# Two bottleneck blocks in f32: the centre taken off behind TensorE's transposes, and VectorE's steps in the Gram stages cut smaller

## The chip, the cores and the metric

The kernel runs on one core of one Trainium2 chip. The metric is the device time of one execution in microseconds (us), and of several executions the median.

## What is computed

The reference applies two residual bottleneck blocks, one behind the other, to x of 64 x 1024 x 14 x 14 in float32. One block is:

```python
out = relu(_bn(_conv(x, w1, b1, 1, 0), g1, be1))      # 1x1, 1024 -> 256
out = relu(_bn(_conv(out, w2, b2, 1, 1), g2, be2))    # 3x3, 256 -> 256
out = _bn(_conv(out, w3, b3, 1, 0), g3, be3)          # 1x1, 256 -> 1024
out = softplus(residual_scale)[0] * out
out = relu(x + out)
```

`_bn` is a batch norm with the mean and variance of the batch itself, over images and pixels. So each block needs the statistics of every convolution's output before it can go on. For the third convolution the kernel doesn't form all outputs twice: their mean and variance follow from the mean of its 256 input channels and from their 256 x 256 matrix of second moments (the Gram matrix), taken over all 64 x 196 = 12544 pixels.

## The kernel before

All 256 channels of the middle tensor, y, lie in SBUF: 128 partitions, two slots (s = 0, 1) of 12544 pixels. A block runs in stages: first convolution, second convolution, the Gram stage (`gram`), statistics of the third convolution (`conv3_stats`), then the third convolution with the residual, in the first block interleaved with the next block's first convolution. TensorE (PE) multiplies, ScalarE (ACT) evicts and applies the norm, VectorE (DVE) adds, GpSimd (POOL) adds and issues some DMAs, SyncE (SP) issues the other DMAs.

The change touches `gram` alone, which runs once per block. It has to do three things for each pixel: apply the second norm and the ReLU in place (`norm` on ScalarE, or `norm_vector` in two steps on VectorE), take off a guess of the channel's mean (`less`: `minus_c`, one number per channel, is added; sums of squares are more exact about a centre), and bring pixels from the free dimension to the partitions, since TensorE contracts over partitions. A transposed pair of chunks, 256 pixels by 256 channels, goes into a tile `zt` (six in turn, each with a column of ones for the mean), and four matmuls into the banks `cp` (g0) and `ap` (g1) add its products. There are 49 pairs, and two ways to transpose one:

- `by_tensor(a)`: four TensorE transposes into a PSUM bank, then VectorE copies the bank to `zt` (line 1046). This serves the first `FIRST` = 7 pairs, while no other data is ready.
- `by_vector(x, i)`: VectorE's stream transpose turns blocks of 32 x 32 (line 1052). The blocks have to lie right first, so DMAs spread 1536 pixels (a step) over a second buffer, a home: 16 DMAs a step, four runs of pixels by four groups of partitions, seven on POOL's queue and nine on SP's (line 1032). There are two homes, used in turn (named `ws` and `home` in the first block's trace, both `home` in the second's), and seven steps of six pairs each. Step 0 takes the pixels 768 to 2303, so that TensorE's pairs 3 to 6 take those from 2304 on.

Pair i's matmuls stand behind the transposes of pair i + 1 in PE's program. PE, DVE and ACT execute in the order in which the program lists their instructions; here the order is written out by hand (`tc.keep_in_program_order`). `pairs` lists it: after the pairs 1 and 5 of TensorE the steps 0 and 1 are spread, after step k the step k + 2, into the same home. `norm_to(end)` norms and centres whole pieces of pixels up to `end`, mostly 1568 long, whenever a spread needs them; so six stream transposes stand in a row on VectorE, and then two `less` of 1568. A pad matmul (`busy`, into the bank `ax`) stands behind the first pair's transposes.

Of the kernel before, what the change touches and what calls it, by code (L numbers as in the profile page):

```python
# [52 lines left out]
NPX = N * HW  # L53
CH = 2
NZT = 6

FIRST, LAST = 7, 0
RUN = 3 * P
STEP = 4 * RUN
STEPS = (NPX - (FIRST + LAST) * CH * P) // STEP  # L60

LAG = 14

# [3 lines left out]
GPX = GI * HW  # L67
# [20 lines left out]
def bottlenecks(ctx: ExitStack, tc: tile.TileContext, x, w1s, w2s, w3s, pars, out):  # L88
    nc = tc.nc
# [5 lines left out]
    y_all = keep.tile([P, MS, NPX], FP, tag="y", name="y")  # L95
# [70 lines left out]
    def matmul(*args, **kw):  # L166

        tc.keep_in_program_order(nc.tensor.matmul(*args, **kw))  # L168

    def busy(psum, tag, n, with_=None):  # L170

        v = ident if with_ is None else with_
        for i in range(n):
            matmul(psum.tile(448, tag), v, v[:, :1].to_broadcast([P, 448]), start=True, stop=True)
# [154 lines left out]
    def act(*args, **kw):  # L329

        tc.keep_in_program_order(nc.scalar.activation(*args, **kw))  # L331
# [662 lines left out]
    def gram(psum, pool, homes, aff, minus_c, beside):  # L994

        g0, g1 = psum.tile(M + 1, "cp"), psum.tile(P + 1, "ap")
        zts = [pool.tile([P, CH, M + 1], FP, tag=f"zt{i}", name=f"zt{i}") for i in range(NZT)]
        for zt in zts:  # L1000
            nc.gpsimd.memset(zt[:, :, M:], 1.0)
        zts = itertools.cycle(zts)

        head = 3 * CH * P
        start = FIRST * CH * P
        bounds = [0, CH * P, head, head + STEP, *range(2 * GPX, NPX + 1, GPX)]
        pieces = list(zip(bounds, bounds[1:]))

        def less(s, y):
            tc.keep_in_program_order(nc.vector.tensor_scalar(y, y, minus_c[:, s : s + 1], None, ALU.add))  # L1010

        def norm_to(end):

            while pieces and pieces[0][0] < end:
                a, e = pieces.pop(0)
                for s in reversed(range(MS)):
                    y = y_all[:, s, a:e]
                    if a == 0 and s == 1:
                        norm_vector(s, y, aff, minus_c[:, s : s + 1])
                    else:  # L1020
                        norm(s, y, aff)
                        less(s, y)

        def spread(k):

            first = start + k * STEP if k else head
            norm_to(first + STEP)
            x = homes[k % 2][:, : MS * STEP].rearrange("p (s j f) -> p s j f", s=MS, j=4)
            for i, j in itertools.product(range(4), range(4)):
                queue = nc.gpsimd if 4 * i + j in (1, 3, 6, 8, 10, 13, 15) else nc.sync  # L1030
                a = first + i * RUN
                queue.dma_start(out=x[32 * i : 32 * i + 32, :, j], in_=y_all[32 * j : 32 * j + 32, :, a : a + RUN])
            return x.rearrange("p s j f -> p (s j) f")

        def by_tensor(a):
            tp = psum.tile(CH * M)
            for c in range(CH):
                for s in range(MS):
                    tc.keep_in_program_order(
                        nc.tensor.transpose(  # L1040
                            tp[:, (c * MS + s) * P : (c * MS + s + 1) * P],
                            y_all[:, s, a + c * P : a + (c + 1) * P], ident,
                        )
                    )
            zt = next(zts)
            tc.keep_in_program_order(nc.vector.tensor_copy(zt[:, :, :M], tp.rearrange("p (c m) -> p c m", c=CH)))  # L1046
            return zt

        def by_vector(x, i):
            zt = next(zts)  # L1050
            tc.keep_in_program_order(
                nc.vector.transpose(
                    zt[:, :, :M].rearrange("p b (n c) -> p b n c", c=32),
                    x[:, :, i * CH * 32 : (i + 1) * CH * 32].rearrange("p n (b r) -> p b n r", r=32),
                )
            )
            return zt

        def pairs():

            norm_to(head)
            then = {
                1: lambda: ready.append(spread(0)),
                2: partial(norm_to, 2 * GPX),
                4: partial(norm_to, 3 * GPX),
                5: lambda: ready.append(spread(1)),
            }
            for i in range(FIRST):
                a = i * CH * P
                yield by_tensor(a if a < head else a + STEP)  # L1070
                if i == 0:
                    busy(psum, "ax", 1)
                if i in then:
                    then[i]()
            for k in range(STEPS):
                x = ready.pop(0)
                for i in range(RUN // (CH * 32)):
                    yield by_vector(x, i)
                if k + 2 < STEPS:
                    ready.append(spread(k + 2))  # L1080
            norm_to(NPX)
            for i in range(LAST):
                yield by_tensor(NPX - (LAST - i) * CH * P)

        ready = []
# [239 lines left out]
    ident = keep.tile([P, P], FP, tag="ident", name="ident")  # L1325
# [6 lines left out]
    with tc.tile_pool(name="first", bufs=1) as one, tc.tile_pool(  # L1332
        name="first_x", bufs=4
    ) as xpool, ExitStack() as scope:
        psum = Psum(scope, ["ps"], ps=4, ay=2)
        w1 = load_w1(one, 0, nc.scalar)
        pair = [load_x(xpool, 0, t, CS if t == 0 else 2) for t in range(2)]
        for b in range(2):
            p = keep.tile([P, NPAR], FP, tag=f"par{b}", name=f"par{b}")
# [14 lines left out]
        pieces = list(itertools.product(range(2), range(MS), range(MS)))  # L1354
# [16 lines left out]
    for b in range(2):  # L1371
        pb = par[b]
        minus_c = keep.tile([P, MS], FP, tag="minus_c", name="minus_c")
# [5 lines left out]
        with tc.tile_pool(name=f"last_{b}", bufs=1) as one, tc.tile_pool(  # L1379
            name=f"last_x_{b}", bufs=4 if b == 0 else 5  # L1380
# [4 lines left out]
            aff = affine(aggregate(stats2, 0), pb, G2, BE2)  # L1385
            with ExitStack() as scope:
                if b == 0:
                    psum = Psum(scope, ["cy", "ay", "cx", "cy", "ay"], cy=2, ay=2)
                else:
                    psum = Psum(scope, ["cy", "cx"], cy=2, cx=2, cp=2)  # L1390
                with tc.tile_pool(name=f"gram_{b}", bufs=1) as pool:
                    def x_tile(name):
                        return xpool.tile([P, CS * PX], FP, tag="x", name=name)
# [3 lines left out]
                    homes = [x_tile("home") if b else ws.rearrange("p i n -> p (i n)"), x_tile("home")]  # L1397
# [17 lines left out]
                aff = affine(mv3, pb, G3, BE3, conv_bias=B3)  # L1415
# [51 lines left out]
```

## Time and profile before

| | us |
|---|---|
| median of 3 runs (1943.93 to 1944.21) | 1944.0 |
| profiled execution, its own time | 1944.06 |
| profiled execution, its span | 1942.3 |
| first Gram stage: from the norm's first step on ACT to the last Gram matmul | 586.49 to 659.93 |
| second Gram stage, the same | 1552.01 to 1624.91 |

The span is the time from the first to the last instruction on the core. The page of the profile gives the busy time of each engine, the chain of work that ended last, the costliest groups of instructions and the DMA issues. Other views used here are the groups by line and shape, the waits of an engine (who waited for whom, total, times, longest), the timeline (start, duration, engine, line, operation, tiles, shapes, count, and in brackets the idle time before and what ended it) and busy times in stretches. A row of the timeline with xN stands for N instructions in a row.

### The profile page before, as it was taken

How to read it: one execution, taken by the hardware profiler on the slowest of the kernel's cores; microseconds unless marked ns; L12 is line 12 of the kernel's file. 1: busy time of each engine (PE TensorE's matmuls, PEld its weight loads, DVE VectorE, ACT ScalarE, POOL GpSimd, SP SyncE). 2: the span in 40 equal slices, each digit the busy share in tenths (PEclk: the TensorE clock that was granted, in tenths of full speed). 3: DMA queues.
4: the chain of work that ended last, by engine and by line, in shares of the span. 5: the costliest groups of instructions: out<-in, count | busy, mean ns of one | idle time of the engine just before them, and what ended most of it. 6: DMA issues, size and time to landing. Idle time of an engine off the chain costs nothing.

```text
span 1942.3 us, 27081 instructions
## 1 busy us (share of the span) xinstructions
PE 1918.6 (99%) x9438; PEld 1612.1 (83%) x9438; DVE 1544.3 (80%) x2473; ACT 1046.2 (54%) x2098; POOL 575.1 (30%) x674
## 2 busy tenths in 40 slices
PE   9999999999999999999999999999999999999999
PEld 5555557999997799999999999989999987555555
DVE  5778667999998667776776767689999975888886
ACT  2222214677765055555555555456777651666666
POOL 0111100212105133433333334302121051666664
PEclk9999999999999999999999999999999999999999
DMA  7777634887948634444444444258788486899998
GB/s 291 273 250 263 235 129 157 204 221 202 230 141 207 197 137 187 175 166 166 181 185 167 166 178 180 108 181 209 215 208 225 140 194 233 279 334 335 333 342 300
DMA packets 201849, 413.91 MB, mean 213 GB/s; under 512 B 37809, under 2 KB 178001, under 8 KB 185201
## 3 DMA queue, kind: packets, MB, share of 16 engines
q1 hardware_dynamic: 161728, 324.66, 49.0%
q0 software_dynamic: 34368, 36.45, 9.3%
q10 hardware_dynamic: 5616, 51.06, 6.3%
q8 instruction: 75, 1.23, 0.3%
q14 instruction: 62, 0.50, 0.1%
HBM read 263.75 MB, written 115.34 MB: 195 GB/s over the span
## 4 chain that ended last, share of the span: by engine, by line
PE 92%; DVE 5%; DMA 1%; ACT 1%; issue 1%; SPq 0%; POOL 0%; DVEq 0%; ACTq 0%
PE cy L168 17%; PE ay L168 17%; PE columns L168 13%; PE cp L168 12%; PE ap L168 10%; PE m L168 6%; PE l L168 6%; PE cx L168 5%; PE ax L168 4%; PE ps L168 1%; DMA home<-y 1%; ACT y L544 1%; DVE v L628 0%; DVE sums L622 0%; DVE steps L697 0%
## 5 line engine op out<-in xcount | busy, mean ns | idle before, releaser
L331 ACT ACTIVATE cu<-cy,scale 128x196 f32<-128x196 f32 (+1 forms) x552 | 256.7, 474 | 277.5 <-PE cy L168 271.3
L168 PE MATMUL columns<-v,ub 128*128 128x224 f32 (+1 forms) x1536 | 300.7, 337 | 0.0
L331 ACT ACTIVATE x<-x,shift 128x392 f32<-128x392 f32 x428 | 241.1, 613 | 59.5 <-POOL x L490 53.1
L168 PEld LDWEIGHTS columns<-v,ub 128*128 128x128 f32 x1536 | 269.2, 188 | 2.8
L464 DVE SCALAR_TENSOR_TENSOR x<-cp,scale,x 128x196 f32<-128x196 f32 (+1 forms) x368 | 178.2, 484 | 97.2 <-PE cp L168 96.1
L168 PE MATMUL cy<-ct,ws 128*128 128x196 f32 (+1 forms) x736 | 221.9, 383 | 1.1 <-ACT cu L331 1.1
L485 POOL TENSOR_TENSOR x<-x,cu 128x196 f32<-128x196 f32 (+1 forms) x184 | 159.3, 866 | 172.1 <-ACT cu L331 162.5
L168 PE MATMUL ay<-at,ws 128*128 128x196 f32 (+1 forms) x752 | 209.1, 381 | 0.0
L490 POOL TENSOR_TENSOR x<-x,cu 128x392 f32<-128x392 f32 x124 | 125.9, 1016 | 192.8 <-DVE x L464 188.1
L168 PEld LDWEIGHTS ay<-at,ws 128*128 128x128 f32 x752 | 136.5, 190 | 33.4
L168 PEld LDWEIGHTS cy<-ct,ws 128*128 128x128 f32 x736 | 133.3, 190 | 36.4 <-ACT cu L331 4.2
L168 PE MATMUL l<-diffs,ub 128*128 128x224 f32 (+1 forms) x768 | 149.1, 337 | 2.6 <-PE columns L168 2.6
L511 POOL TENSOR_TENSOR x<-x,cu 128x392 f32<-128x392 f32 x120 | 121.9, 1017 | 85.9 <-DVE x L464 62.4
L168 PE MATMUL m<-sums,ua 128*128 128x224 f32 (+1 forms) x752 | 145.9, 337 | 1.5 <-DVE sums L622 1.5
L168 PEld LDWEIGHTS l<-diffs,ub 128*128 128x128 f32 x768 | 134.3, 189 | 4.4 <-PE columns L168 3.9
L331 ACT ACTIVATE au<-ay 128x196 f32<-128x196 f32 (+1 forms) x141 | 53.8, 381 | 155.2 <-PE ay L168 152.4
L464 DVE SCALAR_TENSOR_TENSOR x<-cx,scale,x 128x196 f32<-128x196 f32 (+1 forms) x184 | 89.1, 484 | 57.4 <-PE cx L168 57.4
L168 PEld LDWEIGHTS m<-sums,ua 128*128 128x128 f32 x752 | 131.3, 189 | 3.3 <-DVE sums L622 2.9
L168 PE MATMUL cx<-y,w 128*128 128x196 f32 (+1 forms) x404 | 124.1, 392 | 0.4 <-DVE x L1148 0.4
L168 PE MATMUL cy<-y,w 128*128 128x196 f32 (+1 forms) x404 | 123.8, 392 | 0.0
L168 PE MATMUL cp<-zt 128*128 128x257 f32 x392 | 118.0, 382 | 1.8 <-DVE zt L1046 1.7
L168 PE MATMUL cp<-y,ws 128*128 128x196 f32 (+1 forms) x368 | 113.6, 390 | 0.9 <-DVE x L464 0.9
(216 smaller groups left out, 3924.8 us busy)
## 6 DMA issues: line engine op xcount, KB each, us to landing
x<-in_x SPq DMA_DIRECT2D x62, 1568.0 KB, 6.8
ub<-u SPq DMA_DIRECT2D x94, 768.0 KB, 5.2
x<-mid SPq DMA_DIRECT2D x32, 1568.0 KB, 8.2
mid<-x ACTq DMA_DIRECT2D x31, 1568.0 KB, 5.1
out<-x SPq DMA_DIRECT2D x123, 392.0 KB, 5.7
ua<-u SPq DMA_DIRECT2D x94, 256.0 KB, 3.0
u<-y POOLq DMA_DIRECT2D x48, 256.0 KB, 5.8
home<-y SPq DMA_DIRECT2D x90, 96.0 KB, 4.3
```

Source lines behind the costliest of these rows:

```text
L168: tc.keep_in_program_order(nc.tensor.matmul(*args, **kw))
L331: tc.keep_in_program_order(nc.scalar.activation(*args, **kw))
L464: nc.vector.scalar_tensor_tensor(v, bank, self.scale[:, o : o + 1], v, ALU.mult, ALU.add)
L485: nc.gpsimd.tensor_add(self.part(1, 1), self.part(1, 1), u3)
L490: nc.gpsimd.tensor_add(v, v, self.u12)
L511: nc.gpsimd.tensor_add(v, v, self.u12[:, i * self.n : (i + 1) * self.n])
L544: act(y, y, AF.Relu, bias=shift[:, s : s + 1], scale=scale[:, s : s + 1])
```

## The change

Only `gram` and the constant `LAST`, which was 0 and goes, are edited. The pieces of pixels that are normed and centred are cut differently and put elsewhere in the order:

- TensorE transposes its pairs before they are centred. Two new matmuls and a copy make `c_row`, a tile that holds `minus_c` as a row on all partitions, and VectorE's copy of the bank becomes an addition of that row. The pixels of these pairs are centred in y itself later, during the steps 1 and 2.
- Step 0 is normed, centred and spread in two halves (`move(0, range(2))`, `move(0, range(2, 4))`). Slot 1 of the pixels of TensorE's pairs 3 to 6 is normed by VectorE, in two pieces of 512.
- Pieces are steps of 1536 pixels. During step k, `less` for the step k + 2 stands behind the first and the second stream transpose, slot 1 and slot 0, instead of both behind the sixth. The `less` of the pixels that TensorE transposed stand behind the third and the fourth transpose of steps 1 and 2. `move(k + 2)` still stands behind the sixth.

The new code with its order, cut to that:

```diff
-        bounds = [0, CH * P, head, head + STEP, *range(2 * GPX, NPX + 1, GPX)]
-        def norm_to(end):
-            while pieces and pieces[0][0] < end:
-                a, e = pieces.pop(0)
-                for s in reversed(range(MS)):
-                    y = y_all[:, s, a:e]
-                    if a == 0 and s == 1:
-                        norm_vector(s, y, aff, minus_c[:, s : s + 1])
-                    else:
-                        norm(s, y, aff)
-                        less(s, y)
...
+        def center_row():
+            ps = psum.tile(M, "ax")
+            for s in range(MS):
+                matmul(
+                    ps[:, s * P : (s + 1) * P], minus_c[:, s : s + 1].to_broadcast([P, P]), ident, start=True, stop=True
+                )
+            tc.keep_in_program_order(nc.vector.tensor_copy(c_row, ps))
...
-            tc.keep_in_program_order(nc.vector.tensor_copy(zt[:, :, :M], tp.rearrange("p (c m) -> p c m", c=CH)))
+            tc.keep_in_program_order(
+                nc.vector.tensor_add(
+                    zt[:, :, :M], tp.rearrange("p (c m) -> p c m", c=CH), c_row[:, None, :].to_broadcast([P, CH, M])
+                )
+            )
...
-            norm_to(head)
-            then = {
-                1: lambda: ready.append(spread(0)),
-                2: partial(norm_to, 2 * GPX),
-                4: partial(norm_to, 3 * GPX),
-                5: lambda: ready.append(spread(1)),
-            }
+            at = head + STEP
+            half = (start + STEP - at) // 2
+            normed_by_vector(0, px, 1)
+            normed(0, px, (0,))
+            center_row()
+            normed(px, head)
+            def then(i):
+                if i == 0:
+                    busy(psum, "ax", 1)
+                elif i == 1:
+                    normed(head, middle)
+                    less(head, middle, (1,))
+                elif i == 2:
+                    less(head, middle, (0,))
+                    move(0, range(2))
+                    normed(at, at + half, (0,))
+                    normed_by_vector(at, at + half, 1)
+                    normed(middle, at)
+                elif i == 3:
+                    less(middle, at)
+                    move(0, range(2, 4))
+                    normed(at + half, start + STEP, (0,))
+                    normed_by_vector(at + half, start + STEP, 1)
+                elif i == 4:
+                    normed(start + STEP, start + 2 * STEP)
+                elif i == 5:
+                    less(start + STEP, start + 2 * STEP)
+                    move(1, range(4))
...
                 for i in range(RUN // (CH * 32)):
                     yield by_vector(x, i)
+                    a = start + (k + 2) * STEP
+                    if i < MS and k + 2 < STEPS:
+                        normed(a, a + STEP, both[i : i + 1])
+                        less(a, a + STEP, both[i : i + 1])
+                    elif 2 <= i < 2 + MS and k in (1, 2):
+                        less(*((0, head), (at, start + STEP))[k - 1], (i - 2,))
                 if k + 2 < STEPS:
-                    ready.append(spread(k + 2))
+                    move(k + 2, range(4))
```

`px` is 256, `head` 768, `middle` 1536, `start` 1792, `at` 2304 and `half` 512. `normed` calls `norm` on ScalarE for the given slots, slot 1 first; `normed_by_vector` calls `norm_vector` for one slot.

More of the change, by code (lines that the diff above doesn't have):

```diff
@@ L55 @@
 NZT = 6
-FIRST, LAST = 7, 0
+FIRST = 7
 RUN = 3 * P
 STEP = 4 * RUN
-STEPS = (NPX - (FIRST + LAST) * CH * P) // STEP
+STEPS = (NPX - FIRST * CH * P) // STEP
 LAG = 14
@@ L1002, in gram @@
         zts = itertools.cycle(zts)
-        head = 3 * CH * P
-        start = FIRST * CH * P
-        bounds = [0, CH * P, head, head + STEP, *range(2 * GPX, NPX + 1, GPX)]
-        pieces = list(zip(bounds, bounds[1:]))
-        def less(s, y):
-            tc.keep_in_program_order(nc.vector.tensor_scalar(y, y, minus_c[:, s : s + 1], None, ALU.add))
-        def norm_to(end):
-            while pieces and pieces[0][0] < end:
-                a, e = pieces.pop(0)
-                for s in reversed(range(MS)):
-                    y = y_all[:, s, a:e]
-                    if a == 0 and s == 1:
-                        norm_vector(s, y, aff, minus_c[:, s : s + 1])
-                    else:
-                        norm(s, y, aff)
-                        less(s, y)
@@ L1024, in spread, with normed, normed_by_vector, less @@
-        def spread(k):
+        px = CH * P
+        head = 3 * px
+        start = FIRST * px
+        middle = head + STEP // 2
+        both = tuple(reversed(range(MS)))
+        def normed(a, e, slots=both):
+            for s in slots:
+                norm(s, y_all[:, s, a:e], aff, act)
+        def normed_by_vector(a, e, s, less=0.0):
+            norm_vector(s, y_all[:, s, a:e], aff, less)
+        def less(a, e, slots=both):
+            for s in slots:
+                y = y_all[:, s, a:e]
+                tc.keep_in_program_order(nc.vector.tensor_scalar(y, y, minus_c[:, s : s + 1], None, ALU.add))
@@ L1026, in spread, with home, move @@
+        def home(k):
+            return homes[k % 2][:, : MS * STEP].rearrange("p (s j f) -> p s j f", s=MS, j=4)
+        def move(k, runs):
             first = start + k * STEP if k else head
-            norm_to(first + STEP)
-            x = homes[k % 2][:, : MS * STEP].rearrange("p (s j f) -> p s j f", s=MS, j=4)
-            for i, j in itertools.product(range(4), range(4)):
+            for i, j in itertools.product(runs, range(4)):
                 queue = nc.gpsimd if 4 * i + j in (1, 3, 6, 8, 10, 13, 15) else nc.sync
@@ L1031, in spread @@
                 a = first + i * RUN
-                queue.dma_start(out=x[32 * i : 32 * i + 32, :, j], in_=y_all[32 * j : 32 * j + 32, :, a : a + RUN])
-            return x.rearrange("p s j f -> p (s j) f")
+                queue.dma_start(
+                    out=home(k)[32 * i : 32 * i + 32, :, j], in_=y_all[32 * j : 32 * j + 32, :, a : a + RUN]
+                )
+        c_row = pool.tile([P, M], FP, tag="c_row", name="c_row")
+        def center_row():
[5 more added lines that the diff above has]
+            tc.keep_in_program_order(nc.vector.tensor_copy(c_row, ps))
@@ L1045, in by_tensor @@
             zt = next(zts)
-            tc.keep_in_program_order(nc.vector.tensor_copy(zt[:, :, :M], tp.rearrange("p (c m) -> p c m", c=CH)))
+            tc.keep_in_program_order(
+                nc.vector.tensor_add(
+                    zt[:, :, :M], tp.rearrange("p (c m) -> p c m", c=CH), c_row[:, None, :].to_broadcast([P, CH, M])
+                )
+            )
             return zt
@@ L1059, in pairs @@
         def pairs():
-            norm_to(head)
-            then = {
-                1: lambda: ready.append(spread(0)),
-                2: partial(norm_to, 2 * GPX),
-                4: partial(norm_to, 3 * GPX),
-                5: lambda: ready.append(spread(1)),
-            }
-            for i in range(FIRST):
-                a = i * CH * P
-                yield by_tensor(a if a < head else a + STEP)
+            at = head + STEP
+            half = (start + STEP - at) // 2
+            normed_by_vector(0, px, 1)
@@ L1071, in pairs @@
+            normed(0, px, (0,))
+            center_row()
+            normed(px, head)
+            def then(i):
                 if i == 0:
                     busy(psum, "ax", 1)
-                if i in then:
-                    then[i]()
+                elif i == 1:
[17 more added lines that the diff above has]
+                    move(1, range(4))
@@ L1075, in pairs @@
+            for i in range(FIRST):
+                a = i * px
+                yield by_tensor(a if a < head else a + STEP)
+                then(i)
             for k in range(STEPS):
-                x = ready.pop(0)
+                x = home(k).rearrange("p s j f -> p (s j) f")
                 for i in range(RUN // (CH * 32)):
                     yield by_vector(x, i)
-                if k + 2 < STEPS:
-                    ready.append(spread(k + 2))
-            norm_to(NPX)
-            for i in range(LAST):
-                yield by_tensor(NPX - (LAST - i) * CH * P)
@@ L1085, in gram @@
-        ready = []
+                    a = start + (k + 2) * STEP
[4 more added lines that the diff above has]
+                        less(*((0, head), (at, start + STEP))[k - 1], (i - 2,))
+                if k + 2 < STEPS:
+                    move(k + 2, range(4))
         total = NPX // (CH * P)
```

## The prediction

> **What bounds the kernel now.** First the page: which engine has no idle time, and whose work the chain that ended last consists of.
>
> ```profile
> PE 1918.6 (99%) x9438; PEld 1612.1 (83%) x9438; DVE 1544.3 (80%) x2473; ACT 1046.2 (54%) x2098; POOL 575.1 (30%) x674
> ...
> PE 92%; DVE 5%; DMA 1%; ACT 1%; issue 1%; SPq 0%; POOL 0%; DVEq 0%; ACTq 0%
> ```
>
> TensorE (PE) sets the time. An edit to the two Gram stages (584 to 660 us and 1550 to 1625 us) can only win PE's idle time there. So second, PE's waits in 582 to 660:
>
> ```profile
> PE cy L1040 <- DVE y L1010: 1.4, 1, 1.4
> PE cp L168 <- DVE zt L1046: 0.8, 1, 0.8
> PE cy L1040 <- PE m L168: 0.5, 1, 0.5
> ```
>
> The second stage gives the same three numbers: 2.7 us per stage. Not all can be won. A pair of transposed chunks costs PE 1.31 us (in the chain: cp 0.43 and ap 0.22, twice), six pairs (one step through a home buffer) 7.88 us. Third, the timeline of VectorE (DVE) behind the last TensorE pair, and SP's beside it:
>
> ```profile
> 602.53 3.68 DVE L1052 STREAM_TRANSPOSE zt<-ws 128x512 f32<-128x512 f32 x6
> 606.13 1.94 DVE L1010 TENSOR_SCALAR y<-y,minus_c 128x1568 f32<-128x1568 f32 x2
> 611.24 3.68 DVE L1052 STREAM_TRANSPOSE zt<-home 128x512 f32<-128x512 f32 x6 [3.17 <-DMA home<-y]
> 614.85 1.94 DVE L1010 TENSOR_SCALAR y<-y,minus_c 128x1568 f32<-128x1568 f32 x2
> 619.48 3.68 DVE L1052 STREAM_TRANSPOSE zt<-ws 128x512 f32<-128x512 f32 x6 [2.69 <-DMA home<-y]
> 623.08 1.94 DVE L1010 TENSOR_SCALAR y<-y,minus_c 128x1568 f32<-128x1568 f32 x2
> 625.43 3.71 DVE L1052 STREAM_TRANSPOSE zt<-home 128x512 f32<-128x512 f32 x6 [0.41 <-DMA ws<-y]
> ```
> ```profile
> 592.71 6.30 SPq L1032 DMA_DIRECT2D ws<-y  x9
> 599.51 6.32 SPq L1032 DMA_DIRECT2D home<-y  x9
> 606.24 6.48 SPq L1032 DMA_DIRECT2D ws<-y  x9
> 614.95 6.21 SPq L1032 DMA_DIRECT2D home<-y  x9
> ```
>
> Here lies a second bound, just under PE: each step's DMAs start 0.1 us after the sixth transpose that read the same home (614.95 after 611.24 + 3.68). Home to home again, the loop is 611.24 to 625.43 = 14.2 us (step 1 to 3), 619.48 to 633.83 = 14.4 (2 to 4); in the second stage 14.8 (1576.02 to 1590.84) and 15.0 (1582.54 to 1597.52). PE needs 15.76 for two steps: the margin is 0.8 to 1.6 us. The subtractions (1.94 us) come behind the sixth transpose, beside the DMAs, and lengthen the loop by nothing.
>
> **What the Trainium skill says.** "VectorE: DVE Perf Modes", Mode 2×_2P: an f32 tensor_scalar in SBUF makes two results a cycle, an operand in PSUM forbids it. The trace agrees: a subtraction of 1536 takes 1.02 us, the copy of 512 out of PSUM 0.69. "SBUF — State Buffer", in the box on DVE blocking DMA: GpSimd can't write DMA descriptors during such a two-port operation. It agrees: POOL's issues take 539 ns in the median and up to 1357 ns, the long ones beside subtractions. "DMA: Bandwidth & Descriptors", Issuing engines are not separate DMA queues: all queues share 16 engines. The windows from 596 to 616 show a DMA share of 1.05 to 1.10 at 203 to 232 GB/s.
>
> **The change, part by part** (times of the first stage; the second is the same 965.5 us later).
>
> 1. *Subtraction leaves the first pair's path.* Before, PE's first transposes (587.79) waited for L1010 after pads that ended at 587.32 (583.76 + 3.56). Now PE first makes the center row there: two matmuls of 128 columns at 0.22 (the row ap, 129 columns) = 0.44, to 587.76; transposes 0.44. DVE copies the row out: 0.43 (the row g<-cp, 257 columns), starting some 0.26 behind the matmul as the copies do behind transposes, to 588.45. The pad matmul writes the same bank ax and now waits for that copy, which it didn't before; with it queue the second pair's transposes: 588.5 + 0.76 = 589.3, where they were at 589.08. The first Gram matmul comes at 589.75 (589.72 before). Gain 0; bounds -0.3 to +0.3.
>
> 2. *tensor_add in place of the copy.* The same 512 elements at one per cycle; the row f<-columns,ls (896 elements, 1.09 us) scales to 0.69. Cost 0, within 0.1 either way.
>
> 3. *Pair 3.* Before: transposes at 594.45, behind four subtractions. Now DVE does add 2 (to 592.45), a subtraction of 768 (0.53 start to start, from 832 at 0.56), then two tensor_scalars on 512 (0.49 each) that norm and are new on DVE: to 593.95. PE starts at 594.0: 0.45 won, 1.2 us of wait left.
>
> 4. *Pairs 4 to 6.* The subtractions of 2 x 0.95 ahead of pairs 5 and 6 shrink to one such block. Adding up, Gram pair 6 starts at 601.45 instead of 602.63: 1.2 us won per stage, if nothing else binds. That is what the restructured norm buys; ScalarE, 512-wide pieces earlier, stays busy to about 611 and off the path.
>
> 5. *Transfers.* Order on SP (63 per stage) and POOL (49) is unchanged, only waits move. The first home: half its DMAs go at 593.0 (behind the subtraction of 768; 592.71 before), the rest at 596.45, SP being busy till then; its last issue is at 598.4 as before, so the first stream transpose stays near 602.7. Gram pair 7: 603.45 against 603.94. Of 1.2, 0.5 is left. The second home waits for a whole 1536 subtracted: 600.8 against 599.51. From issue to transpose took 11.7 here and 10.7 in the second stage (from POOL's 1565.30); POOL is no longer beside subtractions. I take 611.9 for step 1 (611.24 before), bounds 611.2 to 612.6.
>
> 6. *Subtractions between transposes.* Now two of 1536 stand between the first three transposes of steps 0 to 4, two of 768 more in step 1, two of 1024 in step 2. So the sixth transpose ends later by 1.9 us (two at 0.95), in step 1 by 1.9 + 2 x 0.53 = 2.9, in step 2 by 1.9 + 2 x 0.65 = 3.2. Behind it, on SP and POOL, queue all 16 DMAs for that home. The cover of the old subtractions was the DMA time; it is gone. Loops: steps 1 to 3 become 14.2 + 2.9 = 17.1 (17.7 in the second stage), 2 to 4 17.6 to 18.2, against PE's 15.76. Less overlap of homes lets the engines serve one faster; what that gives back no row shows. Lower bound 0, upper 1.5 (steps 4 to 6, the least crowded, took 13.5 and 14.1); I take 0.7.
>  So step 3 comes at 611.9 + 17.1 - 0.7 = 628.3, in the second stage at 611.6 + 17.7 - 0.7 = 628.6 on this clock. Its first pair follows 0.75 later: 629.05 and 629.35. Where PE is starved, the two interleaved subtractions delay the next two pairs (0.6 + 0.95 + 0.67 is over PE's 1.31): 0.2 + 0.24 = 0.44. With 24 pairs to go (31.5) the stage ends at 661.0 and 661.3, against 659.93 and 659.4 (1624.91): +1.1 and +1.9. The later homes stay just inside: step 4 by 636.5, its first pair, 0.75 behind, due at 637.4.
>
> Sum: +3.0 us. The profiled execution took 1944.06 (span 1942.3 and 1.8 around it); the median of the three runs shown is 1944.0. So 1947.0. What I can call a difference here is about 0.2%, 3.9 us.
>
> **Rivals.**
> *A, the forecast (0.58):* the home loop becomes the bound for one round: +1 to +6, so 1945 to 1950. For: the loop's margin of 0.8 to 1.6 is less than the 2.9 to 3.2 added. Against: PE was 2.0 us behind step 3's transposes here (25th pair due at 628.1), and the DMA's give-back is unknown.
> *B, the other side (0.22):* the lighter DMA traffic gives back 1.5 us or more per loop, landing never starves PE, and the head's 1.2 per stage stays, with 0.5 for the wait at 620 that step 2's landing causes in the first stage: -2.9, so 1941.1; at most -3.9 if part 1 also wins 0.5 per stage. It decides at step 3: transposes by 627 mean B. For: loops of 13.2 to 13.5 late in the stages. Against: SP alone needs 6.3 us for nine issues, and a landing 4.5.
> *C (0.14):* no give-back, and steps 4 to 6 are late too; 3.5 per stage: 1951.
> *D (0.06):* gains and losses cancel; the change doesn't do what it says for PE: 1944 to 1945.
>
> **Chances.** Slower by over 0.2% (1947.9): 0.4 of A (0.23) and C: 0.37. Faster by over 0.2% (1940.1): a quarter of B, 0.05, and 0.02 for an error in part 5. The rest, 0.56, within. A's own range is 1945 to 1950; the range for 8 in 10 takes in half of B and most of C: 1942.5 to 1951.
>
> **What would show it.** In the changed profile: Gram pair 6 by 601.5; PE's wait in pair 3 down to about 1.2 us; nine SP issues of step 3 starting about 618 instead of 614.95; PE waiting on stream transposes (not on copies or adds) near 612 and 629; POOL's 1357 ns issues gone. It is wrong if SP's step 3 starts before 616, if PE never waits behind 605, or if the stage ends outside 659 to 663.

## The result and the profile after

The changed kernel takes 1947.03 us (median of 20 runs, 1946.13 to 1949.68). The kernel before, run beside it, takes 1944.22 (20 runs, 1943.23 to 1944.86). The ratio is 1.0017, 95% interval 1.0010 to 1.0024: 2.8 us slower. The whole interval lies above 1, though most of it under the 0.2% that the prediction calls a difference. The profiled execution of the changed kernel took 1948.1, which is 1.1 above its median; the last view of this section shows a likely reason. Everything read from traces here, tables too, is from one profiled execution of each kernel.

First the page, busy time and the chain that ended last:

```profile
PE 1923.1 (99%) x9446; PEld 1615.5 (83%) x9446; DVE 1546.3 (79%) x2485; ACT 1045.3 (54%) x2102; POOL 572.6 (29%) x674
...
PE 92%; DVE 4%; DMA 2%; issue 1%; SPq 1%; ACT 0%; POOL 0%; DVEq 0%; ACTq 0%
```

TensorE still sets the time, but in the chain DVE and ACT have each lost one per cent, and DMA and SP's queue each gained one. Second, what PE waits for, in 582 to 662 (first Gram stage; from here on "the first stage") and then in 1542 to 1632 (the second); the columns are total, times and longest:

```profile
PE cp L168 <- DVE zt L1067: 1.1, 2, 0.9
PE cy L1051 <- DVE y L552: 0.8, 1, 0.8
```
```profile
PE cp L168 <- DVE zt L1067: 2.0, 1, 2.0
PE cx L1051 <- DVE y L552: 0.8, 1, 0.8
```

L1067 is the stream transpose. Before, PE waited 2.7 us per stage, for subtractions (1.4), for the copy of a TensorE pair (0.8) and behind its own pads (0.5); now 0.8 is left, in pair 3, and 1.1 and 2.0 us of waiting for stream transposes are new. In the first stage this view shows less waiting than before, although the stage ends 1.07 us later (at 661.00): it leaves out the short gaps in front of single pairs, which the table below counts. Where the waits lie is in PE's timeline, first stage:

```profile
594.04 0.55 PE L1051 MATMUL cy<-ident,y 128*128 128x128 f32 x3 [0.81 <-DVE y L552]
...
601.35 0.70 PE L168 MATMUL cp<-zt 128*128 128x257 f32 x2
...
603.87 0.70 PE L168 MATMUL cp<-zt 128*128 128x257 f32 x2 [0.94 <-DVE zt L1067]
...
636.67 0.70 PE L168 MATMUL cp<-zt 128*128 128x257 f32 x2 [0.19 <-DVE zt L1067]
```

These are pair 3's transposes and the Gram pairs 6, 7 and 31. Pair 6 comes 1.28 us earlier than before (602.63), pair 7 only 0.17 (604.04): it is the first pair of home 0. Pair 31 is the first of step 4. VectorE and SP beside it:

```profile
603.10 0.71 DVE L1067 STREAM_TRANSPOSE zt<-ws 128x512 f32<-128x512 f32 x1 [1.80 <-DMA home<-y]
...
610.03 0.71 DVE L1067 STREAM_TRANSPOSE zt<-home 128x512 f32<-128x512 f32 x1 [1.40 <-DMA home<-y]
...
615.33 1.30 DVE L1067 STREAM_TRANSPOSE zt<-home 128x512 f32<-128x512 f32 x2
619.26 0.71 DVE L1067 STREAM_TRANSPOSE zt<-ws 128x512 f32<-128x512 f32 x1 [2.63 <-PE ap L168]
...
626.63 0.71 DVE L1067 STREAM_TRANSPOSE zt<-home 128x512 f32<-128x512 f32 x1 [0.50 <-DVE zt L1067]
...
635.90 0.71 DVE L1067 STREAM_TRANSPOSE zt<-ws 128x512 f32<-128x512 f32 x1 [3.71 <-DMA home<-y]
```
```profile
593.09 5.94 SPq L1031 DMA_DIRECT2D ws<-y  x9
600.72 6.59 SPq L1031 DMA_DIRECT2D home<-y  x9
608.66 6.05 SPq L1031 DMA_DIRECT2D ws<-y  x9
616.65 6.91 SPq L1031 DMA_DIRECT2D home<-y  x9
626.16 6.25 SPq L1031 DMA_DIRECT2D ws<-y  x9
```

Read the two fences together. Step 1's six transposes take from 610.03 to 616.63 (615.33 + 1.30), 6.60 us with four subtractions between them, where they took 3.68; SP's spread into that home follows at 616.65. Home to home the loop is now 626.63 - 610.03 = 16.6 us (step 1 to 3) and 635.90 - 619.26 = 16.6 (2 to 4), more than the 15.76 that PE needs for two steps. In brackets at 619.26 stands PE: VectorE waits there for a free `zt`, PE is behind. At 635.90 stands a DMA: the reserve is used up, and PE waits. The distance of two transposes has grown too: with a subtraction of 1536 between them VectorE starts one every 1.5 us (603.10, 604.62 and 606.15 in the same timeline), while PE asks for one every 1.31.

To compare kernels, add up by how much the distance of two Gram pairs' starts exceeds 1.314 us. The first column holds 2.2 us of TensorE's own transposes in every kernel (five times 0.44); the rest is idle time, or work at a lower clock. The first number of each field is the first stage's, the other the second's.

| us lost | pairs 1 to 6 | pair 7 | pairs 8 to 48 |
|---|---|---|---|
| before | 5.03 / 5.02 | 0.10 / 0.10 | 0.54 / 0.00 |
| after | 3.57 / 3.58 | 1.21 / 2.26 | 1.80 / 1.97 |

Of the first stage's 1.80, only 0.35 is lost at pair 31, to a home that lands late. The other 1.45 are lost in pairs for which the home is there: the pairs 8 to 10 (0.52), 20 to 22 (0.42) and 32 to 34 (0.53), which VectorE delivers too far apart once PE has no reserve.

Last, the windows of the second stage around pair 7 (1571.15); behind the five engines' busy times come PE's granted clock, the DMA share and GB/s:

```profile
1569.00:1571.00 2.00, 0.16 (x2) 0.00 (x0) 0.62 (x1) 2.00 (x3) 1.94 (x4) 1.00 0.87 230
1571.00:1573.00 2.00, 1.85 (x8) 1.62 (x9) 2.00 (x4) 2.00 (x2) 0.00 (x0) 0.75 0.89 257
1573.00:1576.00 3.00, 3.00 (x13) 2.58 (x13) 2.92 (x5) 3.00 (x3) 0.00 (x0) 0.60 0.54 147
```

Behind 2.0 us of idle the granted clock is halved for 3.4 us (1571.99 to 1575.41 in the trace's clock record). The pairs 8 and 9 lose 0.65 and 1.13 there, where a starved home otherwise costs its second and third pair 0.21 each: 1.36 us more. That is the larger part of the table's 1.97, and about what lies between this execution (1948.1) and the median. That the other runs over 1948 have the same cause is not shown; e9 tried.

### The profile page after: what moved, and what is told of

It reads as the page before. It is cut to its first block, busy times and chain, and to the rows that moved or that the text cites. A ratio compares the mean times of both kernels' runs of the same rounds, so it can differ in the third digit from the quotient of the medians.

```text
span 1946.3 us, 27100 instructions
## 1 busy us (share of the span) xinstructions
PE 1923.1 (99%) x9446; PEld 1615.5 (83%) x9446; DVE 1546.3 (79%) x2485; ACT 1045.3 (54%) x2102; POOL 572.6 (29%) x674
## 4 chain that ended last, share of the span: by engine, by line
PE 92%; DVE 4%; DMA 2%; issue 1%; SPq 1%; ACT 0%; POOL 0%; DVEq 0%; ACTq 0%
PE ay L168 17%; PE cy L168 17%; PE columns L168 13%; PE cp L168 12%; PE ap L168 10%; PE m L168 7%; PE l L168 6%; PE cx L168 5%; PE ax L168 5%; PE ps L168 1%; SPq L1031 1%; DMA home<-y 1%; DVE y L1020 0%; DMA x<-mid 0%; DMA out<-x 0%
```

## The experiments

The kernel before ran beside all of them: 1944.17 us (52 runs) beside e1 to e4, 1944.16 (57 runs) beside e5, e6, e8 and e9, 1944.36 (22 runs) beside e7. By then the theory was: the head (pairs 0 to 6) has become earlier, but home 0's landing has not, so the gain turns into a wait at pair 7; and the interleaved subtractions make the loop longer than PE's demand, which costs about 2 us. The rivals are a loss by DMA contention or by the head's own new work, whatever the place of the subtractions. No run takes contention away by itself.

### e1: the subtractions behind the transposes again

In the changed kernel each step's subtractions go behind the sixth transpose and its spread, one step further ahead, so that the spread does not wait for them.

```diff
+                elif i == 6:
+                    normed(start + 2 * STEP, start + 3 * STEP)
+                    less(start + 2 * STEP, start + 3 * STEP)
...
-                    if i < MS and k + 2 < STEPS:
-                        normed(a, a + STEP, both[i : i + 1])
-                        less(a, a + STEP, both[i : i + 1])
-                    elif 2 <= i < 2 + MS and k in (1, 2):
-                        less(*((0, head), (at, start + STEP))[k - 1], (i - 2,))
                 if k + 2 < STEPS:
                     move(k + 2, range(4))
+                a = start + (k + 3) * STEP
+                if k + 3 < STEPS:
+                    normed(a, a + STEP)
+                    less(a, a + STEP)
+                elif k + 3 < STEPS + 2:
+                    less(*((0, head), (at, start + STEP))[k + 3 - STEPS])
```

> The changed kernel with the subtractions of the steps taken out from between the stream transposes and put one step ahead, behind the sixth transpose and behind the DMAs that it releases (those of step 2 behind the last TensorE pair, those of the pixels that TensorE transposed behind the last two). Theory 1 (the interleaved subtractions delay the following transposes and the next home's DMAs): six transposes again take 3.7 us, the pairs 8 to 10 no longer lag by 0.2 each, SP's step 3 starts near 614 instead of 616.7; the head's 1.3 us per stage stays in part. About 1943, 1 us under the kernel before and 4 under the changed one. Theory 2 (the later start of the first two homes' DMAs costs the time): within 0.5 us of the changed kernel, 1947.

Measured: 1944.80 us (1944.00 to 1947.25, 13 runs), ratio 1.0004 [0.9995, 1.0012]. 2.2 us against the changed kernel come back, where theory 1 expected 4. VectorE's timeline of e1, first stage:

```profile
600.88 1.99 DVE L1020 TENSOR_SCALAR y<-y,minus_c 128x1536 f32<-128x1536 f32 x2
602.92 3.68 DVE L1067 STREAM_TRANSPOSE zt<-ws 128x512 f32<-128x512 f32 x6
...
611.21 3.68 DVE L1067 STREAM_TRANSPOSE zt<-home 128x512 f32<-128x512 f32 x6 [2.78 <-DMA home<-y]
...
625.25 3.68 DVE L1067 STREAM_TRANSPOSE zt<-home 128x512 f32<-128x512 f32 x6 [1.39 <-DMA ws<-y]
```

Six in a row again, and the loop is 625.25 - 611.21 = 14.0 us, under PE's 15.76. PE loses 0.51 and 0.10 at the pairs 8 to 48, as before the change. But with the loop of before and a head that brings pair 6 to 601.02, e1 is no faster than the kernel before: it loses 1.35 and 1.59 us at pair 7, where home 0's first transpose comes at 602.92 (602.53 before). The head's gain goes there, nearly whole. Two things end together at that point: the last of home 0's DMAs lands at 602.70 by the trace's landing record, and VectorE, which takes its work in order, is busy to 602.87 with the subtractions of step 2 (the first row) that this edit put ahead of home 0. e1 alone can't tell which of them holds pair 7.

### e2: the kernel before with its subtractions between the transposes

```diff
                 for i in range(RUN // (CH * 32)):
                     yield by_vector(x, i)
+                    if i < MS and k + 2 < STEPS and pieces and pieces[0][0] < start + (k + 3) * STEP:
+                        y = y_all[:, MS - 1 - i, slice(*pieces[0])]
+                        norm(MS - 1 - i, y, aff)
+                        less(MS - 1 - i, y)
+                        if i == MS - 1:
+                            pieces.pop(0)
```

> The kernel before with one edit: the two subtractions of 1568 for step k + 2 stand behind the first and the second stream transpose of step k instead of behind the sixth. Theory 1: the sixth transpose ends 1.9 us later in the steps 0 to 3, and wherever the pairs behind a home's landing are waited for they lag by 0.2 to 0.25 twice: +1.5 to +4 us, 1946 to 1948. Theory 2: nothing moves in the transfers' start of the homes 0 and 1, so 1944 to 1944.5.

Measured: 1944.79 (1943.95 to 1946.14, 13 runs), ratio 1.0003 [0.9995, 1.0011]: 0.6 us, between the two theories, and the interval includes 1. VectorE's timeline of e2:

```profile
610.86 0.72 DVE L1052 STREAM_TRANSPOSE zt<-home 128x512 f32<-128x512 f32 x1 [2.54 <-DMA home<-y]
...
626.35 0.71 DVE L1052 STREAM_TRANSPOSE zt<-home 128x512 f32<-128x512 f32 x1 [2.37 <-DMA ws<-y]
```

The loop from step 1 to step 3 grows from 14.2 to 626.35 - 610.86 = 15.5, not by the 1.9 of two subtractions, and so stays just under PE's 15.76; the two further pairs of subtractions, those of TensorE's pixels, are not in this kernel. Also its head is late (pair 6 at 602.81), so that home 0 (602.74) keeps nobody waiting. Not every loop of e2 stays under: from step 3 to step 5 it takes 16.3 us in the first stage (626.35 to 642.60), which costs PE nothing there, and 17.2 in the second (1591.32 to 1608.55), where pair 37, the first of step 5, loses 0.72. So the place of the subtractions is cheap as long as PE has a reserve, and dear where a late home or a long loop has used it up.

### e3: without the pad

```diff
-                if i == 0:
-                    busy(psum, "ax", 1)
-                elif i == 1:
+                if i == 1:
                     normed(head, middle)
```

> The changed kernel without the pad matmul behind the first pair's transposes, which waits for the copy of the center row. The head's transposes of pair 1 come 0.8 us earlier; pair 3 then waits longer for VectorE's norm. Theory 1 and theory 2 both say that home 0 bounds the first pairs of step 0, so within 0.5 us of the changed kernel, 1946.5 to 1947.5. If the head itself bounds, 1 to 1.6 us less.

Measured: 1946.69 (1945.04 to 1948.26, 21 runs), ratio 1.0012 [1.0006, 1.0019]; 0.3 us under the changed kernel, well inside the spread of either. Pair 0 comes at 589.39 instead of 589.89, and pair 7 at 603.50 instead of 603.87: part of it is eaten by the same landings. The pad's new wait for `c_row` is not what makes the change slow.

### e4: step 1 in halves

Step 1 is subtracted and spread in two halves, as step 0 is, so that its DMAs need not wait for 1536 pixels of both slots.

```diff
-                    less(start + STEP, start + 2 * STEP)
-                    move(1, range(4))
+                    less(start + STEP, start + STEP + STEP // 2)
+                    move(1, range(2))
+                    less(start + STEP + STEP // 2, start + 2 * STEP)
+                    move(1, range(2, 4))
```

> The changed kernel with step 1 too subtracted and moved in two halves of 768 pixels, so that its first eight DMAs start about 1 us earlier. Theory 1: step 1 landed before TensorE asked for it, so within 0.5 us of the changed kernel. Theory 2: the later start of home 1 costs 1 us or more per stage, so 1 to 2 us less than the changed kernel.

Measured: 1947.44 (1946.54 to 1950.46, 16 runs), ratio 1.0019 [1.0012, 1.0026], no better than the changed kernel. SP's spread of step 1 starts at 600.45 instead of 600.72, though this stage as a whole began 0.54 later (pair 0 at 590.43 for 589.89), so 0.8 earlier within the stage. Yet step 1 comes at 611.10 instead of 610.03, later even within the stage. Step 1 kept nobody waiting, so an earlier start of it had nothing to win.

### e5: step 0 not centred

> e1_ahead without the subtractions on step 0's pixels (768 to 2303 stay uncentred, a part of the computation left out), so that the DMAs of home 0 can start at about 590.4 instead of 592.8 and the second half at 592.9 instead of 596. If home 0's landing is what takes the head's gain away (pair 6 at 601.0 but pair 7 only at 603.7 in e1_ahead), then the first stream transpose comes near 600.7, PE doesn't wait for it, and 1 to 2 us per stage are won: 1941 to 1942.5. If something else holds the pairs from 7 on (the later homes), it stays at 1944 to 1945.

```diff
                 elif i == 1:
                     normed(head, middle)
-                    less(head, middle, (1,))
                 elif i == 2:
-                    less(head, middle, (0,))
                     move(0, range(2))
...
                 elif i == 3:
-                    less(middle, at)
                     move(0, range(2, 4))
```

Measured: 1942.64 (1941.86 to 1946.76, 13 runs), ratio 0.9993 [0.9985, 1.0002], 2.2 us under e1, from which it differs by this alone. That is just above the range that was expected, and home 0's first transpose, expected near 600.7, moves only to 602.24 and pair 7 to 602.99. PE still waits 0.9 us for it in each stage. The transfers are not the reason:

```profile
600.38 1.94 DVE L1020 TENSOR_SCALAR y<-y,minus_c 128x1536 f32<-128x1536 f32 x2
602.24 3.67 DVE L1067 STREAM_TRANSPOSE zt<-ws 128x512 f32<-128x512 f32 x6
```

The last of home 0's DMAs lands at 599.37 by the landing record (602.70 in e1), and from 600 to 601 the DMA engines are at a share of 0.00. The first transpose follows 2.9 us after this landing, without idle time on VectorE: the subtractions of step 2, which e1's edit put ahead of it, hold it. In the second stage it is the same (landed at 1563.74, transposed from 1566.20). So leaving out the centring brought home 0 early enough, and what held pair 7 after that was VectorE's own order. The expectation looked at the landing alone.

### e6: the head in another order

If home 0 sets the head's end, the remedy is to issue its DMAs earlier. This edit also takes the subtractions of step 2 out of the way of home 0's first transposes. In e1 the subtractions of step 0 go one TensorE pair ahead, step 1's slot 1 behind pair 4 and slot 0 behind pair 5, and step 2's behind the third and fifth transpose of step 0.

```diff
                     busy(psum, "ax", 1)
-                elif i == 1:
                     normed(head, middle)
                     less(head, middle, (1,))
-                elif i == 2:
+                elif i == 1:
                     less(head, middle, (0,))
                     move(0, range(2))
                     normed(at, at + half, (0,))
-                    normed_by_vector(at, at + half, 1)
                     normed(middle, at)
-                elif i == 3:
+                elif i == 2:
+                    normed_by_vector(at, at + half, 1)
                     less(middle, at)
                     move(0, range(2, 4))
+                elif i == 3:
                     normed(at + half, start + STEP, (0,))
                     normed_by_vector(at + half, start + STEP, 1)
-                elif i == 4:
                     normed(start + STEP, start + 2 * STEP)
+                elif i == 4:
+                    less(start + STEP, start + 2 * STEP, (1,))
                 elif i == 5:
-                    less(start + STEP, start + 2 * STEP)
+                    less(start + STEP, start + 2 * STEP, (0,))
                     move(1, range(4))
-                elif i == 6:
-                    normed(start + 2 * STEP, start + 3 * STEP)
-                    less(start + 2 * STEP, start + 3 * STEP)
...
                     yield by_vector(x, i)
+                    if k == 0 and i in (2, 4):
+                        a = start + 2 * STEP
+                        normed(a, a + STEP, (1 - (i - 2) // 2,))
+                        less(a, a + STEP, (1 - (i - 2) // 2,))
```

> e1_ahead with the full computation and another order in the head: the subtractions of step 0 stand one TensorE pair earlier, in the places where VectorE waits for ScalarE or TensorE (slot 1's half ahead of pair 1's addition, and so on), slot 1 of step 1 behind pair 4, and those of step 2 behind the third and the fifth transpose of step 0. Home 0's DMAs start near 591.3 and 594.5, the first transpose at 601 to 601.5, pair 7 at about 602. If home 0 bounds: 1 to 1.7 us per stage under e1_ahead, 1941.5 to 1943. If it doesn't: 1944 to 1945.

Measured: 1941.24 (1940.05 to 1942.83, 21 runs), ratio 0.9985 [0.9979, 0.9992]: 2.9 us under the kernel before, 5.8 under the changed one. VectorE's timeline of e6 and all that PE waits for in its first stage:

```profile
601.06 1.90 DVE L1067 STREAM_TRANSPOSE zt<-ws 128x512 f32<-128x512 f32 x3 [0.85 <-DMA ws<-y]
...
608.75 3.68 DVE L1067 STREAM_TRANSPOSE zt<-home 128x512 f32<-128x512 f32 x6 [0.32 <-PE ap L168]
...
623.76 3.68 DVE L1067 STREAM_TRANSPOSE zt<-home 128x512 f32<-128x512 f32 x6 [0.92 <-PE ap L168]
```
```profile
PE cy L1051 <- DVE y L552: 0.4, 1, 0.4
PE cp L168 <- DVE zt L1067: 0.2, 1, 0.2
```

SP starts home 0 at 591.39 instead of 593.09 in the changed kernel (1.7 us earlier; 592.76 in e1), and its first transpose follows at 601.06 instead of 603.10 (602.92 in e1). In brackets there stands a DMA again: the landing, at 600.84, decides. Pair 7 comes at 601.94, one pair's 1.31 us behind pair 6, without a wait. All that this view has left is 0.6 us.

### e8: that head with the loop of the changed kernel

```diff
-                    if k == 0 and i in (2, 4):
-                        a = start + 2 * STEP
-                        normed(a, a + STEP, (1 - (i - 2) // 2,))
-                        less(a, a + STEP, (1 - (i - 2) // 2,))
+                    a = start + (k + 2) * STEP
+                    if i < MS and k + 2 < STEPS:
+                        normed(a, a + STEP, both[i : i + 1])
+                        less(a, a + STEP, both[i : i + 1])
+                    elif 2 <= i < 2 + MS and k in (1, 2):
+                        less(*((0, head), (at, start + STEP))[k - 1], (i - 2,))
...
-                if k + 3 < STEPS:
-                    normed(a, a + STEP)
-                    less(a, a + STEP)
```

> The head of e6_reordered with the changed kernel's own loop (subtractions between the first transposes, before the next DMAs). If the interleaved subtractions cost what e1_ahead gave back (about 2 us over both stages) whatever the head, this is 2 us over e6_reordered: 1943.5 to 1945. If they cost only where home 0 comes late, as the small cost in e2_before_between suggests (0.6 us), it is within 1 us of e6_reordered.

Measured: 1943.04 (1941.49 to 1944.88, 13 runs), ratio 0.9994 [0.9985, 1.0002]: 1.8 us over e6, where nearly the same edit is worth 2.2 between e1 and the changed kernel. That is just under the range that was expected, and well over the 1 us of the other theory. VectorE's timeline of e8:

```profile
608.59 0.71 DVE L1067 STREAM_TRANSPOSE zt<-home 128x512 f32<-128x512 f32 x1 [2.17 <-DMA home<-y]
...
616.80 0.71 DVE L1067 STREAM_TRANSPOSE zt<-ws 128x512 f32<-128x512 f32 x1 [1.61 <-PE ap L168]
...
625.80 0.71 DVE L1067 STREAM_TRANSPOSE zt<-home 128x512 f32<-128x512 f32 x1 [2.15 <-DMA ws<-y]
```

625.80 - 608.59 = 17.2 us: the loop is over PE's 15.76, and here, where the head is in time, step 3 is the one that PE waits for (pairs 25 to 28 lose 1.12 and 0.87 in the two stages). So the price does not hang on the head; only the home at which it falls due does. Against the changed kernel, which has the same loop, e8 shows the head alone, without step 2's subtractions in the way in either: home 0 lands at 600.67 instead of 602.87, in the second stage at 1564.87 instead of 1570.19, and 4.0 us are won.

### e7: e6 without the pad

```diff
                 if i == 0:
-                    busy(psum, "ax", 1)
                     normed(head, middle)
                     less(head, middle, (1,))
```

> The reordered head with the subtractions one step ahead (e6), and without the pad matmul behind the first pair's transposes. In the changed kernel the missing pad moved the median by 0.3 us (1946.69 against 1947.03), since the time was set by landings and not by the first pairs. In e6 PE waits for no landing at home 0 (pair 7 at 601.94 behind pair 6 without a wait), so what the pad holds back at the first pairs can now come through. Theory 1 (the wait for pair 3's bank or for the norm takes up what the missing pad frees): 1941.0 to 1941.6. Theory 2 (the head bounds from its first pair on): about 0.5 us per stage less, 1940.0 to 1940.5. Theory 3 (PE idles there instead and its clock is granted less): above 1942.

Measured: 1940.59 (1939.66 to 1941.93, 18 runs), ratio 0.9980 [0.9973, 0.9988], the lowest median of all: 3.8 us under the kernel before. Against e6 it is 0.65, a comparison across two batches (1944.16 and 1944.36 for the kernel before, so 0.85 with that taken off). It falls between the ranges of the theories 1 and 2 and rules out theory 3. Pair 0 moves from 589.94 to 589.26, pair 6 from 600.63 to 599.90. Pair 7 loses 0.08 and 0.43: home 0 is just in time.

### e9: one more pad behind Gram pair 6

```diff
+            if k == FIRST:
+                busy(psum, "ax", 1)
```

> The changed kernel with one more pad matmul (0.76 us of PE) behind Gram pair 6, in the time in which PE waits for home 0. If the upper runs of the changed kernel (6 of 20 over 1948) come from the clock that is halved after that wait, as in its profiled execution (0.5 from 1572.0 to 1575.4), the median stays within 0.5 us of 1947 and the runs over 1948 become rarer. If the spread comes from the DMAs' landing itself, it stays as wide.

Measured: 1947.14 (1946.20 to 1948.45, 21 runs), ratio 1.0016 [1.0009, 1.0022]. The median is that of the changed kernel. Of 21 runs, 4 took over 1948, of the changed kernel's 20 it was 6, and the highest is 1948.45 instead of 1949.68: too little to say that the pad keeps the clock up. The mean granted clock that each run lists says a little more: of the 10 runs of both kernels over 1948 six list less than 1.000, of the 31 others three. So a lowered clock goes with a part of the upper runs, but four of them kept 1.000.

Together, the losses of all kernels in the measure of the table above:

| us lost | pairs 1 to 6 | pair 7 | pairs 8 to 48 | median |
|---|---|---|---|---|
| e1 | 3.57 / 3.57 | 1.35 / 1.59 | 0.51 / 0.10 | 1944.80 |
| e2 | 5.03 / 5.01 | 0.10 / 0.10 | 0.17 / 0.98 | 1944.79 |
| e3 | 3.66 / 3.65 | 1.26 / 1.79 | 2.30 / 1.11 | 1946.69 |
| e4 | 3.83 / 3.83 | 1.08 / 2.28 | 1.53 / 1.31 | 1947.44 |
| e5 | 3.04 / 3.04 | 1.16 / 1.16 | 0.10 / 0.51 | 1942.64 |
| e6 | 2.82 / 2.82 | 0.00 / 0.00 | 0.50 / 0.76 | 1941.24 |
| e7 | 2.76 / 2.76 | 0.08 / 0.43 | 0.34 / 0.80 | 1940.59 |
| e8 | 2.81 / 2.82 | 0.03 / 0.00 | 1.78 / 1.50 | 1943.04 |
| e9 | 3.58 / 3.58 | 1.33 / 1.98 | 1.76 / 1.60 | 1947.14 |

The last column but one separates the two loops: wherever the subtractions stand between the transposes with those of TensorE's pixels among them (the changed kernel, e3, e4, e8, e9), 1.1 to 2.3 us per stage are lost there, elsewhere 0.1 to 1.0 (the 0.98 is e2's step 5). The column of pair 7 separates the heads.

## Why the prediction was right, and which steps were not

The median, 1947.03, is within 0.1 us of the 1947.0 forecast. That head and loop would act against each other, and that the loop would win, was right; that the sum came out so near is luck in part, since it agrees better than its terms.

- **Part 1, the first pair.** Forecast 589.75, measured 589.89; the pad did queue for the copy of `c_row`. In the second stage it came at 1556.13, 0.88 behind the 1555.25 of before, since the first stage had ended 1.07 later. e3 and e7 bound what the pad is worth: 0.3 us, and 0.65 where home 0 is in time. Right.
- **Part 2, the addition.** Rows of 0.69 us, as the copies. Right.
- **Part 3.** Pair 3's transposes at 594.04 (forecast 594.0), with 0.81 of wait left instead of 1.2.
- **Part 4.** Pair 6 at 601.35 (forecast 601.45). Right.
- **Part 5, the term that was mis-sized.** Home 0 was to stay at 602.7, because its last issue on SP would stay at 598.4, and leave 0.5 of the 1.2 won. SP's last issue did stay (598.43), but the forecast left out POOL, whose part of the second half now waited for that half's subtraction: POOL's last issue came at 598.45 instead of 596.62. The landing went from 602.31 to 602.87 (in the second stage from 1567.86 to 1570.19, of which 1.07 is the later start of the stage). That POOL's wait is the cause fits, but no run moves it alone. Home 0 came at 603.10, leaving 0.17 at pair 7 in the first stage; in the second, where the table shows 2.26 lost at pair 7 and 1.44 less than before ahead of it, 0.72 was lost. e1 shows this head with the old loop to be worth nothing. Step 1, on the other hand, was forecast at 611.9 and came at 610.03, though SP began it at 600.72 (forecast 600.8): 9.3 us from first issue to first transpose, not 11.1. Before, the next home's spread began 6.7 us behind its own (599.51 to 606.24), now 7.9 (600.72 to 608.66), and the page's median from issue to landing of SP's spreads fell from 4.3 us to 3.9; that less overlap makes a landing faster fits this, but e6 (599.43, the next at 606.63, so 7.2 us apart, and 9.3 us to the first transpose at 608.75) fits it badly, and e2 speaks against it (599.70, the next at 608.34, so 8.6 us apart, and 11.2 us), so the cause is open. "POOL is no longer beside subtractions" holds in part: 22 of its 98 issues took over 600 ns before, 15 do now.
- **Part 6, the loop.** The sixth transpose came later by 2.92 us in step 1 (6.60 for 3.68; forecast 2.9) and by 3.2 in step 2 (626.13 - 619.26 = 6.87). The give-back was 14.2 + 2.9 - 16.6 = 0.5 for steps 1 to 3 and 14.4 + 3.2 - 16.6 = 1.0 for 2 to 4, where 0.7 was taken. A starved home delays its next three pairs by 0.21 + 0.21 + 0.10 = 0.52 (forecast 0.44). The mechanism and the sum of its parts were right, their shares and the place were not. Counted by pairs, the lateness of a home is the small part behind the head (0.35 of the first stage's 1.80), and the transposes spaced too far apart the large one, which the forecast put at 0.44 and counted for one home instead of three. As to the place: since step 1 was 1.9 us earlier than forecast, step 3 (626.63 instead of 628.3) was in time, and PE waited at step 4 instead, which "stay just inside". SP's step 3 started at 616.65, not about 618, and PE waited near 603 and 636, not near 612 and 629.
- **The sum.** Forecast per stage: 0.5 won at the head, 1.6 and 2.4 lost behind it. Measured by the table: 0.35 won and then 0.72 lost at the head, 1.26 and 1.97 lost behind it (0.61 in the second stage without the 1.36 of the halved clock). So the profiled execution lost 4.0 us and not 3.0, and the median 2.8. The two errors of part 5 had opposite signs: home 0 cost about what step 1 saved. No run shows that the two belong together, so this is luck.
- **Readings.** Two numbers that the sum starts from are slightly off. SP's spread follows the sixth transpose by 0.03 us (614.92 to 614.95), not 0.1, and pair 7 stood at 604.04, not 603.94. Neither moves the forecast by more than 0.1 us.

Of the rivals, B (the lighter DMA traffic gives back enough that landings never starve PE) decided at "transposes by 627", and step 3 did come at 626.63. Its claim still fails: PE is starved at homes 0 and 4. The point named for the decision was a poor one, since it looked at one home of a loop that was over PE's demand for several. A, the forecast, holds with another home than it named; of C one home came true, step 4, and there only by 0.19 us of waiting. The 1357 ns issues of POOL are gone (the longest is 1179, the median 539 as before), and the three conditions that would have made the forecast wrong did not come in.

**What the experiments add.** By head and loop, in medians: kernel before 1944.2, with its subtractions between the transposes 1944.8 (e2); the changed head with that 1947.0, with them behind 1944.8 (e1); the reordered head 1943.0 (e8) and 1941.2 (e6). So the place of the subtractions costs 2.2 and 1.8 us in the two newer heads. The head of the change wins nothing until it is reordered, which is worth 3.6 (e1 to e6) and 4.0 (changed kernel to e8). Of both, 1.5 come in the pairs 1 to 6, where the wait in pair 3 halves (0.8 to 0.4 per stage), and 2.9 and 3.4 at pair 7, by the table. At pair 7 the landing is the cause between the changed kernel and e8; between e1 and e6 the landing and VectorE's order changed together.

## What to carry to other kernels

An engine that reaches a transferred buffer earlier gains only what the transfer also gains: find the last issue that this buffer waits for, on every queue, and move that first. Then look whether the buffer is read when it lands: work that stands ahead of the reader in its own engine's order delays it just the same, as in e5. Work placed between the reads of a buffer that is to be refilled is paid by the loop of reading, issuing and landing, and by the distance of the reads themselves. It costs nothing only while both stay under the demand of the bound engine or a reserve covers them; compare them with the demand, for all rounds, not for the one that looks worst. A sum of several terms can come out right with the waits in other places than forecast, so look for each wait where it was said to be.

## What was not expected of the hardware

The Trainium skill, "TensorE: Matmul & The Clock Gate", section What's actually happening, has TensorE go to half its clock after at least one idle window of about 3.4 us. Here the trace shows half clock for 3.4 us behind only 2.0 us of idle, with 0.16 us of PE's work in the two us before pair 7. It did not follow each time: in e4 PE idled just as long at the same place (the first line: start, duration, and in brackets the idle time) and kept its full clock (the second: 1.00 for 1572 to 1574):

```profile
1571.85 0.70 PE L168 MATMUL cp<-zt 128*128 128x257 f32 x2 [2.02 <-DVE zt L1067]
```
```profile
1572.00:1574.00 2.00, 2.00 (x11) 1.70 (x12) 2.00 (x3) 2.00 (x2) 0.00 (x0) 1.00 1.04 239
```

What decides between the two was not tried beyond e9, and stays open. The clock records hold one hint. In all eleven traces the changes of the clock lie whole multiples of 3.413 us apart (in the changed kernel 459, 1 and 108 of them). On this grid the idle time before pair 7 of the changed kernel (1569.16 to 1571.15) lies in one interval, 1568.58 to 1571.99, at whose end the half clock begins. In e4, counted back from its change at 1946.72, a boundary at 1571.26 cuts the idle time (1569.83 to 1571.85) in two. That the place on the grid decides would fit both cases, but two are too few to show it. In the changed kernel's profiled execution, at any rate, a wait of 2 us for a transfer cost 1.4 us more than it lasted.
